# Order of the prefix in a four-layer graph network: edge fetch, row statistics, normalization and the first table products

## The chip, the cores and the metric

The kernel runs on one core of one Trainium2 chip, in one launch. The metric is device microseconds for the whole kernel. Engines are called as the profile calls them: PE (TensorE, matrix products; PEld is its weight load), DVE (VectorE), ACT (ScalarE), POOL (GpSimd) and SP (SyncE, which here only issues DMAs). ACT and POOL issue DMAs too.

## The reference, cut to what matters

A network of four layers works on x (1250 nodes, 512 features, float32) and 21250 edges sorted by target. Each layer adds three sublayers to x: one on the graph, one mixing all nodes, one of experts. The change touches only the start of layer 0, where the graph sublayer and the mixing sublayer read the same normalized x:

```
xn  = (x - mean) / sqrt(var + 1e-5)                    # per row
# graph (GATv2), k = 0, 1, 2; edges with loops, loop attribute = mean of incoming attributes
xl, xr = xn @ Wl[k] + bl[k], xn @ Wr[k] + br[k]        # two tables
m      = leaky_relu(xl[src] + xr[dst] + ef)            # per edge
alpha  = segment_softmax(m @ att[k], dst)
xn     = relu(layernorm(segment_sum(alpha * xl[src], dst) + b_out[k] + xn))
# mixing (linear attention) of the first xn
q, k, v = phi(xn Wq), phi(xn Wk), xn Wv                # phi = elu + 1, 8 heads
out     = (q (k^T v)) / (q . sum(k)) @ W_out + b_out
```

## The kernel before

Rows are kept in ten tiles of 128 (`NT` = 10, the last with 98 rows). x stays in the on-chip memory as `self.x`, `[128, 10, 512]`. A matrix product of one tile with a 512 x 512 weight is four matmuls in the text, each of which the profile shows as two, so eight per product.

**Two arms and a branch.** `count_edges` fetches the edge targets (`dsti`, and shifted by one `nexti`), and counts on DVE how many lie at or above each of 13 block borders (L273) and whether they are sorted (L275). A matmul with ones (L278) adds the counts over partitions into `ps`; L280 copies them to `tot`; L281 to L293 turn them into `flag`, which every engine loads. If it is zero the fast arm runs (`run(True)`), and that is what these inputs do; the other arm is in the program too. Nothing inside an arm can be issued ahead of the branch. `load_x` is called before `count_edges`, so SP issues x's two DMAs (L1571, L1573) ahead of those of the targets (L260, L262).

**The fast arm's first part** is `gat_first`, the function that the change edits most:

- `gat_vectors` and `gat_weights` issue DMAs for att, the weights `wl` and `wr`, and small vectors; L1120 to L1132 are POOL, ACT and SP work on `we` and `br`.
- `prepare_edges` (L314 to L453) assigns edges to 48 groups of 512 in `place_edges`, most of it small DVE instructions; one indirect DMA from POOL's queue (L431) fetches `raw`, the records of all edges; `take_edges` then fills `fields` with some twelve DVE instructions on 48 x 512. `turn_fields` transposes `fields` on PE (L523) into `rec`.
- `ready(t)` computes a tile's row statistics: L205, L206, L207 on DVE, a square root on ACT (L208). `norm_tile` (L221, L222) writes `xn`; L1537 stores it to `xtab` by ACT's DMA queue; `transpose_tile` (L160) writes `xnT`, evacuated by ACT (L134) and DVE (L136) in turn.
- `linear_attention_steps` is a generator. Its first `next` loads `wk`, `wv` and the vector `bo` and makes the K product of tile 0 (L171); later steps are the other K products, sums over nodes (L776), and the Q products, two yields each.
- `gat_tables` gives eight functions per tile, four for the product with `wl` and four with `wr` (L1161); after the fourth of each the result is evacuated (L1169 to L1179) and stored by SP. The local generator `steps` yields after each product: 20 table products, then the rest of the attention.
- `onehot_steps` makes, for each of 47 groups, a one-hot matrix from `rec` on DVE (L550), four transposes (L557) and four small products (L568) on PE, and stores. The loop around it takes one step of `steps` for each group. `clear` (L1721, L1723, L1725) zeroes buffers in memory.
- `mean_edges` (L597 to L633) forms means of the edge attributes, which need all 47 groups.

When all of this is over, other on-chip buffers are opened and `gatv2_fast` begins with indirect DMAs on POOL (L231) that gather table rows per edge.

**What sets the order.** The text is not the order of issue. Every instruction gets a rank from its place in the text; a planner with its own model of costs then writes one queue for each engine, taking at each moment the instruction of best rank that its model says can start. On the chip each engine works through its queue in order and waits where a dependence isn't met yet. So moving lines changes ranks, and the queues follow as far as the planner's model lets them.

Of the kernel before, what the change touches and what calls it, by code (L numbers as in the profile page):

```python
# [25 lines left out]
NT = 10  # L26
# [31 lines left out]
class Net:  # L58
# [193 lines left out]
    def count_edges(self):  # L252


        nc, c = self.nc, self.const
        self.given = c.tile([128, NB], F32, name="given")
        self.before = c.tile([128, NB], F32, name="before")
        with self.tc.tile_pool(name="prep0", bufs=1, side="right") as t1:
            dsti = t1.tile([128, ED], I32, name="dsti")
            nc.sync.dma_start(dsti, self.I["dst1"])  # L260
            nexti = t1.tile([128, ED], I32, name="nexti")
            nc.sync.dma_start(nexti, self.I["dst1n"])  # L262
            dst = t1.tile([128, ED], F32, name="dst")
            nc.vector.tensor_copy(dst, dsti)
            nxt = t1.tile([128, ED], F32, name="nxt")
            nc.vector.tensor_copy(nxt, nexti)
            one = t1.tile([128, ED], F32, name="one")
            nc.vector.memset(one, 1.0)

            cnt = t1.tile([128, NB + 2], F32, name="cnt")  # L270
            junk = t1.tile([128, ED], F32, name="junk")
            for b in range(NB + 1):
                nc.vector.scalar_tensor_tensor(junk, dst, float(b * BN), one, op0=ALU.is_ge,  # L273
                                               op1=ALU.mult, accum_out=cnt[:, b:b + 1])
            nc.vector.scalar_tensor_tensor(junk, dst, 0.0, nxt, op0=ALU.max, op1=ALU.is_gt,  # L275
                                           accum_out=cnt[:, NB + 1:])
            ps = self.tp([128, NB + 2])
            nc.tensor.matmul(ps, lhsT=self.ones, rhs=cnt, start=True, stop=True)  # L278
            tot = t1.tile([128, NB + 2], F32, name="tot")
            nc.vector.tensor_copy(tot, ps)  # L280
            nc.vector.tensor_tensor(self.given, tot[:, :NB], tot[:, 1:NB + 1],  # L281
                                    op=ALU.subtract)

            room = t1.tile([128, NB], F32, name="room")
            nc.vector.memset(room, float(4 * 128 * GE - BN))
            nc.vector.memset(room[:, NB - 1:], float(3 * 128 * GE - (N - (NB - 1) * BN)))
            over = t1.tile([128, NB + 1], F32, name="over")
            nc.vector.tensor_tensor(over[:, :NB], self.given, room, op=ALU.is_gt)
            nc.vector.tensor_copy(over[:, NB:], tot[:, NB + 1:])
            odd = t1.tile([128, 1], F32, name="odd")  # L290
            nc.vector.tensor_reduce(odd, over, AX.X, ALU.add)
            flag = t1.tile([1, 1], I32, name="flag")
            nc.vector.tensor_copy(flag, odd[0:1])  # L293
            nc.vector.tensor_scalar(self.before, tot[:, :NB], tot[:, 0:1], -1.0,
                                    op0=ALU.subtract, op1=ALU.mult)
            return nc.values_load(flag[0:1, 0:1], min_val=0, max_val=128 * ED + NB)
# [1224 lines left out]
    def gat_first(self, pv, xtab):  # L1521
        nc, I = self.nc, self.I
        L = self.gat_vectors(0, pv)
        with self.tc.tile_pool(name="l0", bufs=1) as p, \
                self.tc.tile_pool(name="l0tab", bufs=2) as pt:
            xn = p.tile([128, NT, D], F32, name="xn")
            xnT = p.tile([128, 4, NP], F32, name="xnT")
            with self.tc.tile_pool(name="edge", bufs=1, side="right") as pe, \
                    self.weights(), self.psum(4, 3, 1):
                self.edge_pool = pe  # L1530
                self.gat_weights(L, pt)
                self.prepare_edges()
                for t in range(NT):
                    self.ready(t)
                for t in range(NT):
                    self.norm_tile(t, xn[:, t, :])
                    nc.scalar.dma_start(xtab[t * 128:(t + 1) * 128, :], xn[:, t, :])  # L1537
                    self.transpose_tile(xnT[:, :, t * 128:(t + 1) * 128], xn[:, t, :])
                self.turn_fields(range(6))
                nc.vector.tensor_copy(self.srcI, self.rec[:, :, 0])  # L1540

                attention = self.linear_attention_steps(
                    xn, xnT, I["L0_mix_W_qkv"], I["L0_mix_W_out"], I["L0_mix_b_out"], 1.0,
                    lambda o, d: nc.vector.tensor_scalar(o, d, 1e-6, None, op0=ALU.add))
                next(attention)

                def steps():
                    for t in range(NT):
                        for i, f in enumerate(self.gat_tables(
                                L, pt, t, lambda c: xnT[:, c, t * 128:(t + 1) * 128])):  # L1550
                            f()
                            if i % 4 == 3:
                                yield
                    yield from attention

                steps = steps()
                for i, _ in enumerate(self.onehot_steps()):
                    next(steps, None)
                    if i == 20:
                        self.clear(pt)  # L1560
                self.mean_edges()
                for _ in steps:
                    pass
        with self.psum(4, 2, 2):
            self.gatv2_fast(L, xtab)

    def load_x(self, src):
        nc = self.nc
        nc.vector.memset(self.x[:, NT - 1, :], 0.0)
        main = (NT - 1) * 128  # L1570
        nc.sync.dma_start(self.x[:, :NT - 1, :],  # L1571
                          src[:main, :].rearrange("(t p) d -> p t d", p=128))
        nc.sync.dma_start(self.x[:LAST, NT - 1, :], src[main:, :])  # L1573

    def layer0_ffn(self):
# [1548 lines left out]
```

## Time and profile before

| | us |
|---|---|
| median of 3 runs (lowest to highest) | 4618.6 (4614.17 to 4620.98) |
| the profiled execution | 4626.03 |
| its span | 4624.2 |
| PE busy | 3950.4 (85%) |
| DVE busy | 2760.3 (60%) |
| ACT busy | 1506.7 (33%) |
| POOL busy | 1361.1 (29%) |

The span is the time from the first to the last recorded instruction. Busy shares are means over many stages with different limits; the part in question is the first 312 us, up to the first gather, and the sections below read it by stretches and by the timeline. In the profile's lines a name such as `xn` stands for all tiles of that name, and a line number can be that of a helper (L160, L171, L205) which many callers share. `x<-xn` at L1537 is the store to `xtab`. A matmul's end is modelled, so a busy PE is not PE at its peak.

### The profile page before, as it was taken

To read this page: it belongs to the slowest core of one execution; us is meant where nothing else is said; L and a number is where in the kernel's file an instruction comes from. 1 tells how busy PE (TensorE), PEld (TensorE's weight loads), DVE (VectorE), ACT (ScalarE), POOL (GpSimd) and SP (SyncE) were. 2 spreads that over 40 slices of the span, in tenths; PEclk is the share of its full clock that TensorE was granted. 3 is DMA by queue.
4 is the path that set the end of the run, shared out by engine and by line. 5 is a ranking of instruction groups with operands and counts; after the bars stand their busy time and mean duration, and the time that the engine had idled before them with its cause. 6 is when DMAs were issued, how large, how long until landed. Compare 5 with 4: busy or idle time off the path is not lost.

```text
span 4624.2 us, 49180 instructions
## 1 busy us (share of the span) xinstructions
PE 3950.4 (85%) x15439; PEld 2438.3 (53%) x15454; DVE 2760.3 (60%) x6534; ACT 1506.7 (33%) x2738; POOL 1361.1 (29%) x1198
## 2 busy tenths in 40 slices
PE   6978997899878876799899999997969975898796
PEld 3435553455444443444788877564536553454574
DVE  5358884888488966533796767314693135587301
ACT  2213332343233355111374346222221022455121
POOL 2026663566356501101100000103253003676101
PEclk9998998899989977899999999998989997998798
DMA  6446664566456612411521110382011285565695
GB/s 221 149 124 193 183 190 140 165 185 190 128 168 180 172 63 77 139 33 35 161 65 41 56 34 28 138 318 95 12 54 62 73 271 164 156 202 175 234 339 191
DMA packets 282999, 647.56 MB, mean 140 GB/s; under 512 B 61673, under 2 KB 108905, under 8 KB 267322
## 3 DMA queue, kind: packets, MB, share of 16 engines
q1 hardware_dynamic: 169290, 357.13, 23.7%
q0 software_dynamic: 73088, 234.75, 18.0%
q10 hardware_dynamic: 40352, 52.44, 3.4%
q8 instruction: 126, 2.06, 0.2%
q14 instruction: 143, 1.17, 0.1%
HBM read 528.87 MB, written 120.65 MB: 140 GB/s over the span
## 4 chain that ended last, share of the span: by engine, by line
PE 32%; DVE 9%; DMA 5%; issue 3%; ACT 2%; POOL 1%; SPq 0%; another core or an unknown queue 0%; ACTq 0%; POOLq 0%; DVEq 0%
PE more L2051 5%; PE mm L2601 4%; PE mm L1914 3%; PE mm L179 3%; PE mm L171 3%; PE mm L3039 2%; DMA xe<-routed_in 2%; PE mm L776 2%; PE mm L2295 2%; PE mm L2013 1%; PE more L2877 1%; PE mm L2290 1%; DVE junk L1942 1%; DVE e L1976 1%; PE mm L2405 1%
## 5 line engine op out<-in xcount | busy, mean ns | idle before, releaser
L231 POOL DMA_INDIRECT xl<-xl,srcI x564 | 610.8, 1083 | 404.1 <-PE more L1325 167.6
L1325 PE MATMUL more<-xl,wT 128*128 128x512 f32 x1128 | 584.9, 611 | 5.5 <-ACT wT L1315 5.5
L1256 PE MATMUL mm<-hl,oh 121*128 121x512 f32 x564 | 399.1, 708 | 103.6 <-DVE s L1269 66.7
L1269 DVE TENSOR_TENSOR s<-xl,mm 128x512 f32<-128x512 f32 x540 | 364.0, 680 | 170.2 <-PE mm L1257 80.8
L1272 DVE SCALAR_TENSOR_TENSOR junk<-s,att 128x512 f32<-128x512 f32 x540 | 405.0, 750 | 5.5
L2051 PE MATMUL more<-hh,e 128*128 128x259 f32 x1600 | 384.2, 386 | 11.7 <-ACT o L1994 9.4
L2051 PEld LDWEIGHTS more<-hh,e 128*128 128x128 f32 x1600 | 295.0, 191 | 76.3 <-issue 16.0
L171 PE MATMUL mm<-w,xnT 128*128 128x512 f32 x640 | 307.0, 619 | 13.8 <-DVE xnT L136 5.3
L231 POOL DMA_INDIRECT g<-routed_out,getI x60 | 66.5, 1109 | 681.5 <-DMA routed_out<-o 494.7
L1325 PEld LDWEIGHTS more<-xl,wT 128*128 128x128 f32 x1128 | 207.0, 196 | 92.2 <-issue 44.2
L1257 PE MATMUL mm<-hl,oh 121*128 121x512 f32 x564 | 242.5, 430 | 0.0
L231 POOL DMA_INDIRECT hs<-gcn_h,srcI x188 | 213.5, 1136 | 95.6 <-issue 35.5
L1256 PEld LDWEIGHTS mm<-hl,oh 121*128 121x128 f32 x564 | 112.6, 200 | 226.9 <-issue 115.2
L1243 ACT ACTIVATE oh<-nb 112x512 fp32r<-112x512 bf16 x141 | 88.6, 629 | 356.1 <-DMA nb<-nbt 241.9
L171 PEld LDWEIGHTS mm<-w,xnT 128*128 128x128 f32 x640 | 123.4, 198 | 141.9 <-issue 125.2
L1971 ACT ACTIVATE e<-r,hh 128x512 f32<-128x512 f32 (+1 forms) x240 | 154.1, 646 | 131.8 <-PE more L2051 120.9
L2601 PE MATMUL mm<-form,cw 128*128 128x312 f32 (+1 forms) x640 | 175.5, 436 | 21.8 <-POOL cw L2578 18.2
L2877 PE MATMUL more<-hl,oh 128*128 128x512 f32 x376 | 162.0, 532 | 35.0 <-DVE hl L2838 9.8
L1974 ACT ACTIVATE e<-r,a 128x512 f32<-128x512 f32 (+1 forms) x240 | 152.3, 646 | 70.6 <-DVE e L1976 58.5
L1976 DVE TENSOR_TENSOR e<-e,e 128x512 f32<-128x512 f32 (+1 forms) x240 | 141.6, 596 | 50.9 <-ACT e L1971 44.6
L1315 ACT COPY wT<-tp 128x512 f32<-128x512 f32 x141 | 82.3, 584 | 267.4 <-PE tp L1312 212.8
L160 PE MATMUL tp<-ident,xn 128*128 128x128 f32 x280 | 51.4, 331 | 135.2 <-issue 56.2
(618 smaller groups left out, 7894.0 us busy)
## 6 DMA issues: line engine op xcount, KB each, us to landing
w<-L_ffn_Wp SPq DMA_DIRECT2D x64, 1024.0 KB
w<-L_ffn_table SPq DMA_DIRECT2D x56, 1025.0 KB
neg<-ntab SPq DMA_DIRECT2D x80, 320.0 KB
nb<-nbt SPq DMA_DIRECT2D x141, 128.0 KB
hl<-xr SPq DMA_DIRECT2D x36, 448.0 KB
xr<-tro SPq DMA_DIRECT2D x30, 512.0 KB
xe<-routed_in SPq DMA_DIRECT2D x56, 256.0 KB
routed_out<-o ACTq DMA_DIRECT2D x56, 256.0 KB
```

What stands on the lines that cost most here:

```text
L171: self.nc.tensor.matmul(p, lhsT=xT[:, c, t * 128:(t + 1) * 128], rhs=w[:, c, n0:n0 + n], start=c == 0, stop=c == k - 1)
L231: self.nc.gpsimd.indirect_dma_start(out=out, out_offset=None, in_=table, in_offset=bass.IndirectOffsetOnAxis(ap=idx, axis=0), bounds_check ...
L1256: nc.tensor.matmul(m, lhsT=s, rhs=hl[:K, 0, :], start=True, stop=False)
L1257: nc.tensor.matmul(m, lhsT=s, rhs=hl[:K, 1, :], start=False, stop=not on_pe(i))
L1269: nc.vector.tensor_tensor(o, d["xl"][:, j, :D], s, op=ALU.add)
L1272: nc.vector.scalar_tensor_tensor(junk, s, 0.0, L["att"], op0=ALU.max, op1=ALU.mult, accum_out=d["lg"][:, j:j + 1])
L1325: nc.tensor.matmul(B[b]["y"], lhsT=d["wT"][:, j, :], rhs=d["xl"][:, j, :D], start=k == 0 and j == 0, stop=last and j == GE - 1)
L1971: nc.scalar.activation(e1[:, :n], R[q, k, 0][:, :n], AF.Exp, bias=HH[q][:, s, 256:257])
L1976: nc.vector.tensor_tensor(e1[:, :n], e1[:, :n], e2[:, :n], op=ALU.max)
L2051: nc.tensor.matmul(ys[j], lhsT=e[:, j * 128:(j + 1) * 128], rhs=HH[q][:, s, :], start=s == 0, stop=s == NT - 1)
L2601: nc.tensor.matmul(m, lhsT=g[:, which, c, :], rhs=forms[form][:, c, q % 2, q // 2:q // 2 + n], start=j + c == 0, stop=j + 1 == len(gs) and ...
L2877: nc.tensor.matmul(y, lhsT=oh, rhs=hl[:, i], start=i + j == 0 and not (self.fast and k), stop=last and i + j == GE)
```

## The change

- `load_x` is called inside `count_edges`, after the two DMAs of the targets, and fetches x in three pieces of three tiles and one of the last tile, in place of one piece of nine tiles and one of the last.
- `ready(t)` for all ten tiles stands in `count_edges`, after the matmul that adds the counts and ahead of the copy of its result, in place of its old place in `gat_first` after `prepare_edges`.
- In `gat_first` the ten tiles are normalized, stored and transposed first. Two steps of `steps` follow (`wl` and `wr` of tile 0), the first step of the attention, two more steps (tile 1), and then `prepare_edges`, one more step, `turn_fields` and the copy to `srcI`. Before, `prepare_edges` stood ahead of the statistics, and `turn_fields` and `srcI` ahead of the attention's first step and of all of `steps`.

No arithmetic is added or removed.

```diff
@@ count_edges
             nexti = t1.tile([128, ED], I32, name="nexti")
             nc.sync.dma_start(nexti, self.I["dst1n"])
+            self.load_x(self.I["x"])
             dst = t1.tile([128, ED], F32, name="dst")
...
             nc.tensor.matmul(ps, lhsT=self.ones, rhs=cnt, start=True, stop=True)
+            for t in range(NT):
+                self.ready(t)
             tot = t1.tile([128, NB + 2], F32, name="tot")
@@ gat_first
                 self.gat_weights(L, pt)
-                self.prepare_edges()
-                for t in range(NT):
-                    self.ready(t)
                 for t in range(NT):
                     self.norm_tile(t, xn[:, t, :])
                     nc.scalar.dma_start(xtab[t * 128:(t + 1) * 128, :], xn[:, t, :])
                     self.transpose_tile(xnT[:, :, t * 128:(t + 1) * 128], xn[:, t, :])
-                self.turn_fields(range(6))
-                nc.vector.tensor_copy(self.srcI, self.rec[:, :, 0])
-
                 attention = self.linear_attention_steps(
...
-                next(attention)
 
                 def steps():
...
                 steps = steps()
+                for _ in range(2):
+                    next(steps)
+                next(attention)
+                for _ in range(2):
+                    next(steps)
+                self.prepare_edges()
+                next(steps)
+                self.turn_fields(range(6))
+                nc.vector.tensor_copy(self.srcI, self.rec[:, :, 0])
                 for i, _ in enumerate(self.onehot_steps()):
@@ load_x
-        nc.sync.dma_start(self.x[:, :NT - 1, :],
-                          src[:main, :].rearrange("(t p) d -> p t d", p=128))
+        for t in range(0, NT - 1, 3):
+            nc.sync.dma_start(self.x[:, t:t + 3, :], src[t * 128:(t + 3) * 128, :]
+                              .rearrange("(t p) d -> p t d", p=128))
@@ kernel
-        net.load_x(I["x"])
         with net.psum():
             odd = net.count_edges()
```

## The prediction

> **What bounds the kernel now.** I read the page first, then the busy time in stretches, the timeline of the first 320 us by engine, and the table of waits there. The chain of waits reaches back only to 2215 us, so for the prefix (everything ahead of the first gather of the graph layers) the stretches have to say what sets its end. The stretches (length, busy time per engine with instruction counts, granted clock, DMA share, GB/s):
>
> ```profile
> 0.00:10.00 10.00, 0.00 (x0) 0.00 (x0) 1.88 (x13) 0.00 (x0) 0.51 (x6) 1.00 0.76 260
> 10.00:20.00 10.00, 0.61 (x2) 0.50 (x2) 6.73 (x41) 0.00 (x0) 0.75 (x2) 1.00 0.06 13
> 20.00:30.00 10.00, 0.00 (x0) 0.00 (x0) 7.84 (x46) 2.30 (x6) 3.98 (x5) 1.00 0.93 303
> 30.00:40.00 10.00, 4.36 (x8) 2.23 (x9) 6.99 (x18) 1.09 (x4) 1.18 (x2) 1.00 0.97 257
> 40.00:50.00 10.00, 3.55 (x9) 1.44 (x7) 10.00 (x17) 0.41 (x2) 6.65 (x3) 0.88 0.37 137
> 50.00:60.00 10.00, 8.68 (x35) 5.71 (x36) 9.45 (x18) 2.60 (x5) 8.77 (x7) 0.78 0.50 186
> 60.00:70.00 10.00, 9.38 (x51) 4.95 (x50) 7.08 (x13) 6.32 (x11) 4.75 (x4) 1.00 0.41 145
> 70.00:80.00 10.00, 8.93 (x50) 4.38 (x49) 5.04 (x11) 2.85 (x5) 2.29 (x2) 1.00 0.67 242
> 80.00:250.00 170.00, 170.00 (x718) 83.51 (x717) 62.87 (x119) 48.91 (x89) 0.00 (x0) 1.00 0.49 167
> 250.00:312.00 62.00, 57.24 (x162) 27.07 (x160) 33.16 (x68) 11.22 (x20) 0.96 (x1) 0.94 0.22 57
> ```
>
> The first busy column is TensorE. From 80 to 250 us it is busy 170.00 of 170 us at clock 1.00, while VectorE is busy 62.87: there the prefix is bound by matmuls that follow each other without a gap. Before 80 us TensorE is mostly empty and VectorE is nearly full. So the prefix ends earlier by as much TensorE time as the change fills ahead of 80 us. The timeline gives the marks (start, duration, instruction, the idle time before it and who ended it):
>
> ```profile
> 11.25 0.25 DVE L264 CAST dst<-dsti 128x168 f32<-128x168 int32 x1 [8.31 <-DMA dsti<-dst]
> ...
> 18.38 0.14 DVE L293 CAST flag<-odd 1x1 int32<-1x1 f32 x1
> ...
> 26.31 1.39 POOL L431 DMA_INDIRECT raw<-etab,edgeI  x1 [6.01 <-DVE mr L365]
> ...
> 36.53 0.61 DVE L444 CAST fields<-raw 48x512 f32<-48x512 int32 x1 [3.01 <-DMA raw<-etab,edgeI]
> ...
> 36.73 5.71 PE L171 MATMUL mm<-w,xnT 128*128 128x512 f32 x8 [4.54 <-DMA w<-L_mix_W_qkv]
> ...
> 64.36 1.29 DVE L550 TENSOR_TENSOR ohb<-iota_free,rec 128x512 bf16<-128x512 f32 x2
> ```
> ```profile
> 275.14 1.24 PE L523 MATMUL tp<-ident,fields 48*128 48x48 f32 x8 [4.71 <-DVE fields L621]
> ...
> 312.90 1.03 POOL L231 DMA_INDIRECT xl<-xl,srcI  x1 [42.43 <-DVE big L1191]
> ```
>
> The edge targets arrive at 11.25 behind x's 2.3 MB; the branch opens at 19.3 (POOL L351, DVE L314); wk lands at 36.7; the first one-hot starts at 64.36; the first gather waits for VectorE, which ends the prefix at 312. Everything later hangs on that gather, and I assume it moves with it.
>
> **TensorE time left empty before.** In the plateau a 512-column product (8 matmuls) takes 3.68, so one matmul 0.46. At that speed the work done by 80 us is: one K product 3.7; 40 transposes of xn at 8 in 1.06, 5.3; 24 transposes of fields at 12 in 0.94, 1.9; 38 table matmuls 17.5; five one-hot groups at 0.39 + 0.25, 3.2. Sum 31.6, so 48.4 of the 80 us are lost.
>
> **Fetch order and the branch.** The targets (168 KB) go ahead of x. I take them as landed at about 4 us: at 0.74 a first DMA issues, and the DMA engines carry nothing before about 1.5. The counting of 11.25 to 16.79 (5.5 us) then ends at 9.5 and its matmul (0.6) at 10.1. Ten row statistics at 0.68 + 0.16 + 0.13 = 0.97 cost 9.7 us on VectorE. They stand in the text ahead of the copy of the totals; if they stay ahead of it in VectorE's queue, as I assume where x has landed, the totals begin at 19.8, the flag follows 1.0 later (17.49 to 18.52 now), the branch 0.75 after that: 21.5 instead of 19.3, a loss of 2.2 for everything in the branch that isn't VectorE. Other end: the flag slips in ahead of them and the branch opens at 12. The ten square roots (0.20 each, one table load 1.28) lie beside VectorE's work on ScalarE and cost nothing; without that cover, at most 3.3. x in four DMAs instead of two adds two issues at 0.45 on an SP queue with nothing else to send. The tile of zeros in x costs VectorE 0.48 either way.
>
> [...]
>
> **Weights.** Now wk lands 17.2 us after SP's first issue at 19.54. In between go att (0.26 MB), wl, wr, wk (1.05 each), the raw edge records (0.59) and one 0.26 MB store of xn: 4.25 MB at the 280 GB/s of 20 to 40 us is 15.2. After the change up to ten such stores by ScalarE's queue fall into that time. Lower bound without raw: 17.2 - 2.1 = 15; upper with nine more stores: 17.2 + 2.36 MB / 280 GB/s = 25.6. From 21.8 wk lands between 37 and 47; I take 42, because normalizing tile by tile spreads the stores.
>
> [...]
>
> **Products ahead.** By 42 us TensorE has done the transposes (5.3), wl and wr of tile 0 (7.4): 12.7, so 29.3 is lost. Then K, wl and wr of tile 1 and wl of tile 2 follow: 4 x 3.68 = 14.7, to 57.
>
> **The edges, now later.** VectorE from 21.5: ten norms at 0.12 + 0.55 = 6.7, five evacuations 3.4, att 0.4, to 32. Placing 4.3, raw 10.2 (26.31 to 36.53 now, with the evacuations of the moved products, six at 0.7, inside that wait), the field arithmetic 11.4 (36.53 to 47.9 now), transposes and copies 2.6: the first one-hot at 60.5 instead of 64.4. Cheapest, without POOL beside it (0.67 instead of 1.46 for each L452): 57. Dearest, all of it at the doubled rates: 71. Between 57 and 60.5 TensorE has wr of tile 2 to do; I count half as lost, 1.8, and 1.5 for the start of the one-hots as now (8.93 of 10). Lost in all: 29.3 + 1.8 + 1.5 = 32.6.
>
> **Sum.** 48.4 - 32.6 = 15.8 us. The profiled execution took 4626.0 (span 4624.2), so 4610.2 on it; the median of three, 4618.6, becomes 4602.8. At 170 of 170 busy nothing between gives this back. The last one-hot (252.4 now) moves towards the end by some three products (five table products ahead instead of the 1.75 that TensorE had done by then), 11 us; the chain of means behind it ends at 275 with TensorE stalled 4.7, and 36 us of work follow: covered. What isn't moved by the text stays at nothing: no instruction is added, two DMAs are.
>
> **Rivals.**
> (a) The flag goes ahead of the statistics. For: POOL's memset L1721 (19.75) precedes L431 (26.31) though it is later in the text, so the queues are not in text order. Weights start 9 us earlier, VectorE stays as late as before: some 9 us more than the sum, 4594.
> (b) The one-hots set the end, not the matmuls. For: VectorE's one-hots wait 41.2 us on L568. Then only 64.4 - 60.5 = 3.9 is won: 4615. Against: 170 of 170 busy. A planner that had already filled the queues whatever the text says ends here too.
> (c) Slower: raw's gather is stuck on POOL. In-order behind L1125 (waits for br; 8.82 now) and the ten additions of b to x (L805, 14.0 us) that become ready once the norms are done, but need the bias vector, which lands after wv, 46 to 51 us. If they are queued ahead of L431, it starts at 60 to 65, not 36, or up to 6 later with L1125 (4.0) and L1128 (1.5) there too, and the one-hots at 84 to 95. Products beyond the moved ones cover some 5 of the 24 to 34 more; TensorE loses 19 to 29: 4622 to 4632, middle 4627, likelier above it, since L1125 already waits now. If the planner finds three further products (11 us) ahead of the fields' transposes, which TensorE takes in order, it is 4611 to 4616. It decides when the first one-hot is later than 76 (60.5 + 15.8). Against: raw stands earlier in the text than those additions, and now one addition comes only at 43.44.
>
> **Chances.** Forecast 0.50 (4594 to 4609); (a) 0.15; (b) 0.17; (c) 0.18, mostly its dear end. 0.2% is 9.2 us, about what a measurement of this kernel can tell from no change. All of the forecast and (a) lie below 4609.4: faster 0.65. (b) and the mild end of (c): same 0.22. The rest of (c), above 4627.8: slower 0.13. Range 4590 to 4628: below it only (a) with wk at its earliest, above it the dear end of (c).
>
> **What would show it.** First dst at 4 us, not 11; wl's first product before 35 us; 85% or more of TensorE busy from 42 us on; the first one-hot at 57 to 64; the first gather near 297. A first gather at 312 or later, L431 after 50 us, or a TensorE wait of over 5 us on fields would prove it wrong.

## The result, and the profile after

The changed kernel takes 4621.6 us (median of 19 runs, 4599.4 to 4647.3) against 4623.4 us of the kernel before in the same session (19 runs): ratio 0.9993 (estimated from all runs, so not the quotient of the two medians), 95% interval 0.9978 to 1.0007. In a second session it was 0.9984 (0.9970 to 0.9999). So it is faster by 0.22% at most by the first interval, by 0.30% at most by the second, where 0.34% was forecast; the two ratios stand for gains of 3 and 7 us, not 15.8. The profiled execution of the changed kernel took 4647.3 us (span 4645.5), the longest of its 19 runs; its prefix can be read, its end can't be held against that of before.

Line numbers behind the change have moved by 3 (L1161 is L1164, L431 is L434, L550 is L553, L805 is L808). First the stretches, with the columns as before (TensorE, its weight load, VectorE, ScalarE, POOL, granted clock, DMA share, GB/s):

```profile
20.00:30.00 10.00, 7.68 (x37) 5.23 (x36) 7.32 (x31) 1.80 (x4) 0.00 (x0) 0.83 1.01 364
30.00:40.00 10.00, 5.50 (x16) 2.27 (x13) 4.61 (x20) 1.17 (x2) 3.89 (x3) 0.91 1.03 282
40.00:50.00 10.00, 7.12 (x10) 3.09 (x11) 4.19 (x6) 1.69 (x3) 2.80 (x2) 0.57 0.55 180
50.00:60.00 10.00, 10.00 (x29) 4.40 (x28) 8.03 (x8) 3.39 (x5) 7.30 (x5) 1.00 0.15 37
60.00:70.00 10.00, 6.39 (x31) 3.63 (x30) 8.85 (x14) 2.50 (x5) 6.54 (x4) 0.78 0.43 160
70.00:80.00 10.00, 7.58 (x34) 3.34 (x33) 5.34 (x6) 1.85 (x4) 6.52 (x5) 0.88 0.44 160
80.00:250.00 170.00, 170.00 (x714) 83.69 (x714) 66.42 (x125) 48.76 (x89) 0.00 (x0) 1.00 0.48 168
```

Next to before, TensorE has filled 20 to 60 us (30.3 busy instead of 16.6), but in 60 to 80 us it is less busy than it was (14.0 instead of 18.3), and in 40 to 50 us its granted clock is 0.57. From 80 to 250 us it is full in both. The marks in the timeline:

```profile
2.69 0.25 DVE L265 CAST dst<-dsti 128x168 f32<-128x168 int32 x1 [0.34 <-DMA dsti<-dst]
...
16.40 0.14 DVE L296 CAST flag<-odd 1x1 int32<-1x1 f32 x1
...
42.88 6.49 PE L171 MATMUL mm<-w,xnT 128*128 128x512 f32 x8 [7.38 <-DMA w<-L_mix_W_qkv]
```
```profile
144.67 4.54 PE L779 MATMUL mm<-k,xn 128*128 128x512 f32 x10
```
```profile
283.63 1.23 PE L526 MATMUL tp<-ident,fields 48*128 48x48 f32 x8 [6.29 <-DVE fields L624]
```
```profile
308.22 1.04 POOL L231 DMA_INDIRECT xl<-xl,srcI  x1 [29.13 <-DVE big L1194]
```

The targets are there at 2.69 and the flag at 16.40, 2 us earlier than before. K's product (L171) waits 7.4 us for wk and then takes 6.49. The first sum of the attention over the nodes (L779, one fixed point of TensorE's plateau) comes at 144.67, before at 154.41: 9.7 us ahead. The line of before:

```profile
154.41 4.54 PE L776 MATMUL mm<-k,xn 128*128 128x512 f32 x10
```

At the first gather 4.7 are left (308.22 for 312.90), at the first mixing product of the graph layer (`more<-xl,wT`, L1328) 0.9 (371.78 for 372.64). Where the edges are late is seen on VectorE and POOL:

```profile
42.64 0.68 DVE L447 CAST fields<-raw 48x512 f32<-48x512 int32 x1 [5.44 <-DMA raw<-etab,edgeI]
...
51.97 0.69 DVE L751 SCALAR_TENSOR_TENSOR k<-mm,r 128x512 f32<-128x512 f32 x1 [5.13 <-ACT r L750]
...
53.18 1.75 DVE L453 TENSOR_TENSOR fields<-fields,e 48x512 f32<-48x512 f32 x1
54.86 3.99 DVE L455 TENSOR_TENSOR fields<-raw,m 48x512 f32<-48x512 f32 x2
...
59.38 3.36 DVE L455 TENSOR_TENSOR fields<-raw,m 48x512 f32<-48x512 f32 x2
62.78 1.60 DVE L456 TENSOR_TENSOR fields<-fields,loops 48x512 f32<-48x512 f32 x1
...
66.22 0.68 DVE L553 TENSOR_TENSOR ohb<-iota_free,rec 128x512 bf16<-128x512 f32 x1
```
```profile
32.10 1.40 POOL L434 DMA_INDIRECT raw<-etab,edgeI  x1 [12.77 <-DVE mr L367]
...
52.70 12.80 POOL L808 TENSOR_TENSOR x<-x,b 128x512 f32<-128x512 f32 x7 [7.59 <-DMA b<-L_mix_b_out]
68.97 1.81 POOL L545 TENSOR_TENSOR rest<-rec,parts 128x768 f32<-128x768 f32 x1 [3.46 <-DVE parts L544]
70.73 2.81 POOL L808 TENSOR_TENSOR x<-x,b 128x512 f32<-128x512 f32 x2
73.50 1.80 POOL L547 TENSOR_TENSOR rest<-rest,parts 128x768 f32<-128x768 f32 x1
```

The field arithmetic (L447 to L456) takes 21.7 us, 42.64 to 64.38; before it took 11.4. Between its operations stands K's phi (L751), which waits 5.1 us; and from 52.7 on POOL adds the mixing bias to x (L808) beside it. L453 and L456 take 1.75 and 1.60 instead of 0.65 to 0.67, and POOL's additions 1.83 each (12.80 / 7) instead of 1.26 for one that ran alone. Two lines of before:

```profile
47.27 0.65 DVE L453 TENSOR_TENSOR fields<-fields,loops 48x512 f32<-48x512 f32 x1
```
```profile
48.51 1.26 POOL L805 TENSOR_TENSOR x<-x,b 128x512 f32<-128x512 f32 x1 [3.13 <-DVE rsx L221]
```

In the changed kernel POOL then does two more additions between its two subtractions that split the fields (L545, L547), for which the one-hots' products wait. And wk is late because SP's queue stands still (waits: engine and line, what it waited for, total, times, longest; then the issue of wk, before and in the changed kernel):

```profile
SPq L1125 <- DMA w<-L_gnn_Wr: 4.8, 1, 4.8
SPq L1121 <- DMA w<-L_gnn_Wl: 4.1, 1, 4.1
SPq L1120 <- DMA att<-L_gnn_att: 2.7, 1, 2.7
```
```profile
21.82 0.39 SPq L141 DMA_DIRECT2D w<-L_mix_W_qkv  x1
```
```profile
32.70 0.40 SPq L141 DMA_DIRECT2D w<-L_mix_W_qkv  x1
```

The three waits are those of fetches and stores of 2 to 32 KB, put in SP's queue ahead of wk; each waits until an earlier large fetch has landed. In the trace of this run the DMAs of SP and ScalarE up to 55 us share eight completion semaphores (a semaphore is the counter that tells of a landing): the fetch of `we` waits for and takes over that of att, the fetch of `bl` that of wl, the store of `br` that of wr. The ten stores of xn by ScalarE use up the others. So wk was issued at 32.7, not at 21.8 as before.

### The profile page after: what moved, and what is told of

Its sections match the earlier page's. It is cut to its first block, busy times and chain, and to the rows that moved or that the text cites. A ratio compares the mean times of both kernels' runs of the same rounds, so it can differ in the third digit from the quotient of the medians.

```text
span 4645.5 us, 49184 instructions
## 1 busy us (share of the span) xinstructions
PE 3969.4 (85%) x15439; PEld 2455.6 (53%) x15454; DVE 2766.2 (60%) x6534; ACT 1508.3 (32%) x2738; POOL 1364.4 (29%) x1198
## 4 chain that ended last, share of the span: by engine, by line
PE 39%; DVE 9%; DMA 6%; issue 3%; ACT 2%; POOL 1%; SPq 1%; another core or an unknown queue 0%; ACTq 0%; POOLq 0%; DVEq 0%
PE mm L171 5%; PE mm L179 5%; PE more L2057 5%; PE mm L2607 4%; PE mm L1920 3%; PE mm L3045 2%; DMA xe<-routed_in 2%; PE mm L779 2%; PE mm L2301 2%; PE more L2883 1%; PE mm L2296 1%; PE mm L2019 1%; PE tp L160 1%; DVE junk L1948 1%; DVE e L1982 1%
## 5 line engine op out<-in xcount | busy, mean ns | idle before, releaser
L1328 PE MATMUL more<-xl,wT 128*128 128x512 f32 x1128 | 578.0, 605 | 3.7 <-ACT wT L1318 3.7
L2057 PEld LDWEIGHTS more<-hh,e 128*128 128x128 f32 x1600 | 293.7, 190 | 77.0 <-issue 15.8
L171 PE MATMUL mm<-w,xnT 128*128 128x512 f32 x640 | 307.1, 619 | 16.6 <-DMA w<-L_mix_W_qkv 7.4
L1328 PEld LDWEIGHTS more<-xl,wT 128*128 128x128 f32 x1128 | 205.5, 194 | 87.4 <-issue 41.6
L171 PEld LDWEIGHTS mm<-w,xnT 128*128 128x128 f32 x640 | 123.2, 198 | 144.2 <-issue 119.9
L2883 PE MATMUL more<-hl,oh 128*128 128x512 f32 x376 | 165.8, 545 | 32.6 <-issue 13.5
L1980 ACT ACTIVATE e<-r,a 128x512 f32<-128x512 f32 (+1 forms) x240 | 152.2, 646 | 71.9 <-DVE e L1982 59.7
L1286 PE MATMUL tp<-ident,lg 128*128 128x128 f32 x564 | 95.0, 292 | 86.1 <-DVE lg L1282 58.0
```

Of the source, the lines that this page charges most:

```text
L171: self.nc.tensor.matmul(p, lhsT=xT[:, c, t * 128:(t + 1) * 128], rhs=w[:, c, n0:n0 + n], start=c == 0, stop=c == k - 1)
L1328: nc.tensor.matmul(B[b]["y"], lhsT=d["wT"][:, j, :], rhs=d["xl"][:, j, :D], start=k == 0 and j == 0, stop=last and j == GE - 1)
L2057: nc.tensor.matmul(ys[j], lhsT=e[:, j * 128:(j + 1) * 128], rhs=HH[q][:, s, :], start=s == 0, stop=s == NT - 1)
L2883: nc.tensor.matmul(y, lhsT=oh, rhs=hl[:, i], start=i + j == 0 and not (self.fast and k), stop=last and i + j == GE)
```

## The experiments

Theory: POOL's additions, now beside the edges' chain, and wk's late issue leave TensorE waiting or at a low clock (0.57 from 40 to 50 us); the chain of means takes some of the lead back; what is left is too small for the time to show. Rivals: full DMA engines hold wk back; the shift doesn't reach the end. A mark at the first gather repeats to 1 to 6 us, a time ratio to about 0.0015 (7 us). All marks in us, one profile each; "table matmuls" are those of L1164 (its number differs by a few lines from kernel to kernel) done by 80 us; each ratio is to the kernel before, run beside it.

| kernel | first one-hot | table matmuls | first sum | first gather | first mixing product | ratio to before, 95% |
|---|---|---|---|---|---|---|
| before | 64.4 | 38 | 154.4 | 312.9 | 372.6 | 1 |
| before, again | 64.8 | 37 | 154.8 | 314.1 | 372.4 | |
| changed | 66.2 | 58 | 144.7 | 308.2 | 371.8 | 0.9993 (0.9978 to 1.0007) |
| changed, again | 61.3 | 60 | 143.9 | 306.3 | 369.5 | 0.9984 (0.9970 to 0.9999) |
| before, branch part only | 54.8 | 41 | 152.5 | 312.1 | 370.7 | 0.9985 (0.9970 to 1.0001) |
| changed, weights first | 65.9 | 65 | 141.8 | 304.7 | 362.3 | 0.9980 (0.9963 to 0.9996) |
| changed, means late | 57.4 | 65 | 141.3 | 300.6 | 367.5 | 0.9992 (0.9977 to 1.0007) |
| changed, additions late | 57.5 | 83 | 132.8 | 295.1 | 352.9 | 0.9972 (0.9962 to 0.9982) |
| the same, again | 61.2 | 75 | 136.6 | 300.7 | 359.1 | 0.9957 (0.9940 to 0.9973) |
| weights first, additions late | 55.4 | 87 | 130.8 | 293.8 | 351.7 | 0.9959 (0.9943 to 0.9975) |
| additions late, means late | 61.0 | 75 | 136.4 | 296.4 | 366.7 | 0.9965 (0.9949 to 0.9981) |
| all three | 56.0 | 86 | 131.3 | 291.3 | 358.0 | 0.9967 (0.9951 to 0.9982) |
| before, additions late | 59.0 | 49 | 149.0 | 308.3 | 369.8 | 0.9975 (0.9958 to 0.9992) |
| changed, delayed | 63.2 | 61 | 143.2 | 330.6 | 376.6 | 1.0021 (1.0001 to 1.0042) |

### Both kernels once more

No edit. 

> The changed kernel once more, so that marks of one profile can be told from accidents of one execution. Theory (T): the marks of the prefix are set by the order of the queues and repeat to within 0.5 us: wk's product at 42.9, first one-hot 66.2, first sum of the attention 144.7, first gather 308.2. The lead of 4.7 us over the kernel before at the first gather is real, and what the profiled execution lost after 2300 us (it ended 20 us late) is not repeated. Rival (accident): the profiled execution was slow throughout and this one has its first gather at 297 to 303. Time: 0.999 to 1.001 of the kernel before under T, 0.996 under the rival.

> The kernel before once more, the same question from the other side: first one-hot 64.4, first gather 312.9, first mixing product of the graph layer at 372.6, last gather of the third graph pass at 1602, each within 0.5 us up to the first gather. If the marks behind 372 us scatter by more than 3 us between executions of one kernel, a lead of 3 us there can't be followed by single profiles.

The lead at the first gather repeats: 306.3 and 308.2 against 312.9 and 314.1. But the marks from 40 to 66 us don't repeat to 0.5 us: K's product began at 39.3 here, 42.9 there, as wk landed earlier or later, and the first one-hot followed (61.3 and 66.2). Nor does the first gather, to better than 2 us. The time, 0.9984, lies between what theory and rival gave.

### The branch part alone

```diff
 (before)
+            self.load_x(self.I["x"])      # in count_edges, behind the targets; x in pieces
...
+            for t in range(NT):           # in count_edges, ahead of the totals
+                self.ready(t)
...
                 self.prepare_edges()      # gat_first: order unchanged
-                for t in range(NT):
-                    self.ready(t)
```

> The kernel before with the first half of the change alone: targets fetched first, x in pieces, row statistics ahead of the branch; normalization, products and edges stay in the old order. Theory (T): the branch opens 2 us earlier (17.3, not 19.25) and VectorE has 5 to 8 us less to do between the branch and the edges, so the edges come earlier than in either kernel: raw issued at 24, first one-hot at 60 to 62, first gather 309 to 311; all of that half's gain is kept, and the second half (products ahead) adds 2 to 3 us at the first gather. Rival (the second half is the loss): first gather at 306 or earlier, ahead of the full change, so that moving the products cost time. Time: 0.999 to 1.000.

The first one-hot came at 54.8, 10 us earlier than before, and the first gather at 312.1, 1 to 2 us earlier: both theories were off, and early one-hots by themselves are worth little: TensorE had only three more table matmuls done by 80 us (41 for 38). By the time (0.9985) this half can't be told from the whole change in the same session (0.9984). Two lines each of VectorE and POOL, then the cast to srcI in the kernel before:

```profile
47.50 7.35 DVE L1541 CAST srcI<-rec 128x192 int32<-128x192 f32 x1
54.77 1.75 DVE L553 TENSOR_TENSOR ohb<-iota_free,rec 128x512 bf16<-128x512 f32 x1
```
```profile
47.29 1.27 POOL L1131 TENSOR_TENSOR wehl<-we,wehl 3x512 fp32r<-3x512 f32 x1
48.52 7.45 POOL L808 TENSOR_TENSOR x<-x,b 128x512 f32<-128x512 f32 x6
```
```profile
64.11 0.30 DVE L1540 CAST srcI<-rec 128x192 int32<-128x192 f32 x1
```

The cast to srcI, 0.30 us before, takes 7.35 here: it ends when POOL's row of seven operations ends (55.97), but for one us. POOL's stayed at 1.24 each. TensorE waits 7.5 us for the copy of `rec` that VectorE has behind this cast, and its first transposes of one-hots start at 57.1.

### The weights first

```diff
 (changed; gat_weights)
         L["wr"] = self.weight(I["L0_gnn_Wr"][k], 4, D)
+        if early is not None:          # the parts of W_qkv for wk and wv
+            L["kv"] = [self.weight(w, 4, D) for w in early]
         v = p.tile([128, D], F32, tag="v", name="we")
...
 (linear_attention_steps)
-            wk = self.weight(w_qkv[:, D:2 * D], 4, D)
-            wv = self.weight(w_qkv[:, 2 * D:3 * D], 4, D)
+            wk, wv = kv or [self.weight(w_qkv[:, i * D:(i + 1) * D], 4, D) for i in (1, 2)]
```

> The changed kernel with wk and wv put straight behind wl and wr in SP's queue, ahead of the small fetches we, bl and br that wait there for earlier DMAs. The same bytes flow, the xn stores included. Theory (T, the queue held wk back): wk is issued at 22 to 25 us instead of 32.7, its product starts at 35 to 38 instead of 42.9, its phi on VectorE is done before the raw records land (42.6), so the 5.1 us that VectorE waited there are gone: first one-hot at 60 to 62 instead of 66.2, first sum of the attention at 138 to 141 instead of 144.7, first gather 302 to 305. Rival (the DMA engines are full: share 1.01): wk lands at 41 to 44 wherever it stands in the queue, and all marks stay as in the changed kernel within 1 us; then wl or wr land later instead. Time: 0.997 to 0.999 under T, 0.999 to 1.001 under the rival.

The queue was the cause, not full engines: with the same bytes wk was issued at 21.7 and its product took 3.70 after a wait of 0.56, where the changed kernel has 6.49 after 7.38, while the products of wl began when they did there (26.3 and 26.2). The kernel with the weights first and the additions late, whose K product began at 36.13, has a DMA share of 1.02 from 20 to 40 us, the changed one 1.01 and 1.03. But the one-hots came no earlier. The K product on TensorE, POOL's additions and what follows them, ScalarE's copy of wehl, and TensorE's wait:

```profile
35.91 3.70 PE L171 MATMUL mm<-w,xnT 128*128 128x512 f32 x8 [0.56 <-DMA w<-L_mix_W_qkv]
...
44.53 16.42 POOL L807 TENSOR_TENSOR x<-x,b 128x512 f32<-128x512 f32 x10 [8.21 <-DMA b<-L_mix_b_out]
60.92 1.25 POOL L1129 TENSOR_TENSOR we<-we,br 3x512 f32<-3x512 f32 x1
```
```profile
62.20 0.62 ACT L1131 CAST wehl<-we 3x512 fp32r<-3x512 f32 x1 [18.53 <-POOL we L1129]
...
64.34 0.66 PE L526 MATMUL tp<-ident,fields 48*128 48x48 f32 x4 [10.84 <-ACT rec L134]
```

All ten additions now stand ahead of the sum that wehl needs (L1129): ScalarE waits 18.5 us for it, with the evacuation of a field transpose queued behind, and TensorE is empty for 10.8 us. The second wait took the place of the first. The first gather (304.7) and the time are as the theory had them, the first sum (141.8) is just past it.

### The additions late

```diff
 (changed; linear_attention_steps, ahead of the loop over the tiles)
             Q, QT = {}, {}
+            if added is None:
+                nc.vector.scalar_tensor_tensor(bo, ks, 0.0, bo, op0=ALU.mult, op1=ALU.add)
```

> The changed kernel with the ten additions of the bias vector to x on POOL made to wait until the attention's column sums ks are there: one VectorE operation (0.7 us) writes b + 0*ks in place of b. Nothing else moves in POOL's queue. Theory (T: POOL's additions beside VectorE's field arithmetic doubled it, L455 at 2.0 and 1.7 each, L453 and L456 at 1.6 to 1.75): L455 takes 1.0 each, L456 0.7, the casts L546 and L548 0.55 instead of 1.6, and POOL's subtractions L545 and L547 come without the additions between them; first one-hot 3 to 6 us earlier than in the changed kernel (56 to 61), TensorE busy 31 of the 40 us up to 80 becomes 34 or more, first sum of the attention at 140 to 142 instead of 144, first gather 303 to 305. Rival (VectorE's durations have another cause, such as the transfers): L455 stays at 1.7 to 2.0 and no mark moves. Second rival: the additions only move the trouble to 220 to 280 us, where POOL's gather of the means (L617) stands behind them: TensorE's stall at 283 grows over 7 us. Time: 0.997 to 0.999.

In this kernel the ten additions of L808 move behind POOL's subtractions, and the order on SP, ScalarE and TensorE stays the same up to the graph layer. VectorE, then POOL:

```profile
48.99 0.68 DVE L453 TENSOR_TENSOR fields<-fields,e 48x512 f32<-48x512 f32 x1
49.59 2.04 DVE L455 TENSOR_TENSOR fields<-raw,m 48x512 f32<-48x512 f32 x2
...
52.15 2.05 DVE L455 TENSOR_TENSOR fields<-raw,m 48x512 f32<-48x512 f32 x2
54.24 0.68 DVE L456 TENSOR_TENSOR fields<-fields,loops 48x512 f32<-48x512 f32 x1
...
57.46 0.68 DVE L553 TENSOR_TENSOR ohb<-iota_free,rec 128x512 bf16<-128x512 f32 x1
...
62.05 0.56 DVE L546 CAST parts<-rest 128x768 bf16<-128x768 f32 x1 [1.93 <-POOL rest L545]
...
64.53 0.56 DVE L548 CAST parts<-rest 128x768 bf16<-128x768 f32 x1 [1.32 <-POOL rest L547]
```
```profile
60.20 1.81 POOL L545 TENSOR_TENSOR rest<-rec,parts 128x768 f32<-128x768 f32 x1 [14.97 <-DVE parts L544]
62.69 1.80 POOL L547 TENSOR_TENSOR rest<-rest,parts 128x768 f32<-128x768 f32 x1 [0.67 <-DMA l0moe_in<-zero]
...
201.22 13.65 POOL L810 TENSOR_TENSOR x<-x,b 128x512 f32<-128x512 f32 x10 [136.72 <-DVE b L806]
```

L453 and L456 are back at 0.68, the casts L546 and L548 at 0.56, and POOL's subtractions follow each other 2.5 us apart, not 4.5. L455 stays at 1.02, so that part of its length isn't POOL's. The additions cost nothing at 201 us, and TensorE's stall in the tail is 6.26 us, not more. The table products by 80 us, changed kernel and this one (matmuls, busy time, mean ns of one):

```profile
L1164 PE MATMUL mm<-w,xnT 128*128 128x512 f32 x58 | 30.7, 669 | 0.0
```
```profile
L1166 PE MATMUL mm<-w,xnT 128*128 128x512 f32 x83 | 38.7, 603 | 0.0
```

25 matmuls more, at 0.47 us each by busy time (38.7 / 83) instead of 0.53 (30.7 / 58); the means of the view are longer because matmuls overlap (83 of 0.603 are 50.0 us, in 38.7 busy). First sum and first gather:

```profile
132.81 4.54 PE L779 MATMUL mm<-k,xn 128*128 128x512 f32 x10
```
```profile
295.12 1.03 POOL L231 DMA_INDIRECT xl<-xl,srcI  x1 [27.84 <-DVE x L185]
```

That is more than the theory said (140 to 142 and 303 to 305): it named the splitting, but its 3 to 6 us were for the first one-hot, ahead of it. The first gather is 17.8 us ahead of before, and the time 0.9972. The repetition:

> The changed kernel with the additions late once more, for a narrower interval beside the other three on one chip: first gather at 294 to 297, first mixing product at 351 to 358, time 0.9965 to 0.998. If the first gather is back at 304 or later, the first run's marks were an accident of one execution, and POOL's additions aren't the cause.

With wk late in this execution (TensorE waited 7.1 us for it, 3.6 in the first), the marks are 4 to 6 us later, past the expected ranges. From the first sum on they are still 5 us or more ahead of the changed kernel; the first one-hot is not (61.2 for 61.3 to 66.2). The time is 0.9957, below the expected range. Against the changed kernel's two ratios the two of this kernel are lower by 0.0012 to 0.0036, 6 to 17 us, with intervals that touch.

### Weights first and additions late

The diffs are those of the two sections above, together.

> Both edits together: wk and wv fetched straight behind wl and wr, and POOL's ten additions made to wait for ks. With the weights first alone, TensorE was busy 25 to 52 us, and then empty for 13 us (52 to 65): the right table's evacuation waited on ScalarE for wehl, which waited on POOL behind all ten additions (16.4 us, 44.5 to 61), and the one-hots were no earlier (65.9). Theory (T: each of the two alone leaves the other's wait standing): first one-hot at 53 to 57, TensorE empty for under 5 us between 25 and 80 us, first sum of the attention at 133 to 137 (144 in the changed kernel, 141.8 with weights first), first gather 296 to 300; that is the gain that the prediction put on the change (15.8 us at the first gather, of 312.9), with the stall of the means still in it. Rival (they overlap: the one-hots or the raw records set the pace): first sum at 139 or later, first gather 301 or later. Time: 0.9955 to 0.9975 under T.

All marks are as expected or earlier. TensorE is empty for 3.5 us between 25 and 80 us. Against the additions late alone the first sum gains 2 to 6 us, the time nothing that can be told (0.9959).

### The means late

```diff
 (changed; mean_edges)
-            self.turn_fields((2, 3))
+            if not self.fast:
+                self.turn_fields((2, 3))
...
 (gat_first)
                 for _ in steps:
                     pass
+                self.turn_fields((2, 3))
```

> The changed kernel with the transposes of the two mean fields (L526, which waited 6.3 us on VectorE's L624 with TensorE idle behind them) moved behind the last attention product. Theory (T: nearer the end the chain of means is no longer covered): the stall of 6.3 us at 283 us and the low clock after it (0.53 in 280 to 290) are gone; first gather at 299 to 302 instead of 306.3 to 308.2, of which the first gather keeps all. Rival (something else holds the end: the means' own gather and VectorE's fields are needed by the first gather or by what follows at once): first gather stays at 305 to 308, or moves and the first mixing product of the graph layer stays at 369 to 372. Time: 0.9965 to 0.9985 under T, as the changed kernel (0.9984) under the rival.

The transposes wait no longer, and the first gather is at 300.6:

```profile
299.64 0.69 PE L526 MATMUL tp<-ident,fields 48*128 48x48 f32 x8
```

Part of that is an early first sum (141.3). The fair measure is the stretch from first sum to first gather: 158.5 and 159.3 before, 163.6 and 162.4 changed, 159.3 here. So the means' stall took back 3 to 5 us, net of a wait of 3.9 us for q (L160 at 285.62) that stands in its place. But the first mixing product is at 367.5, 67 us after the gather (58.2 to 59.7 before, 63.2 and 63.6 changed), and the time is 0.9992: the part of the theory that all of it is kept fell.

> The changed kernel with the additions late and the transposes of the two mean fields behind the last attention product. With the additions late alone TensorE still waited 6.3 us on the means' fields (at 272 us) and the stretch from the first sum of the attention to the first gather was 162.3 us, as in the changed kernel (162.4 to 163.5; before 158.5 to 159.3; with the means late 159.3). Theory (T: the means' stall is worth 3 to 4 us of this stretch): first sum at 132 to 134, first gather 290 to 293, stretch 158 to 160. Rival (something else of the attention's end sets it, such as the copies of q): stretch 162 or more. Time: 0.9955 to 0.9975.

The stretch is 160.0, as expected; the first sum was late (136.4, wk again landed late), and again the first mixing product came late, 70 us after the gather.

> All three edits on the changed kernel: wk and wv straight behind wl and wr, additions late, transposes of the mean fields last. Theory: they add up, as each takes away a wait of its own: first sum of the attention at 130 to 132, first gather 288 to 291, first mixing product of the graph layer at 345 to 350 (before 372.5). Rival (the first mixing product is held by transfers that don't move): 352 or later. Time: 0.995 to 0.997.

First gather 291.3, the earliest of all, but the first mixing product 67 us later, at 358.0: past the rival's 352. (That transfers hold it, the rival's reason, isn't shown.) In all three kernels with this edit that stretch is 67 to 70 us; in the four other profiles with the weights first or the additions late on the changed kernel it is 57.6 to 58.4. What the edit wins at the gather is lost on the way to that mark. Which wait does it, I haven't isolated.

### The same edit on the kernel before

The diff is that of the additions late, applied to the kernel before.

> The kernel before with the same single edit as in the changed kernel: POOL's ten additions of the bias vector to x wait until the attention's ks is there. It asks whether the 11 to 13 us that the edit brought in the changed kernel belong to the edit alone or to the edit and the change together. Theory (T: the change laid the edges' chain, VectorE's field arithmetic and the splitting of the fields, beside those additions; before, most of them fell beside the normalization, 48 to 63 us, and ended before POOL's subtractions L542 at 68.7): the field arithmetic loses some 2 us (L452 1.0 each, not 1.6) and the normalizations their doubled rows (1.3 to 0.53, some 4 us), so first one-hot at 58 to 61 instead of 64.4 and first gather 307 to 310 instead of 312.9 to 314.1; time 3 to 6 us less (0.9985 to 0.9995). So of the changed kernel's 12 to 13 us at the first gather, 7 or more are the change's own, that the additions had hidden. Rival (the edit is a gain of its own): first gather at 302 or earlier, 0.9975 or less, and the change is worth little with or without it.

The marks are where the theory put them: first one-hot 59.0, first gather 308.3. The time, 0.9975, lies at the rival's bound, with the theory's 0.9985 inside its interval. By the marks, then, the additions cost 5 to 6 us at the first gather in the kernel before and 6 to 13 in the changed one, and with them out of the way the change brings the first gather from 308.3 to 295.1 and 300.7, 8 to 13 us. By the time, 0.9957 and 0.9972 against 0.9975, that rest is not settled: the intervals overlap.

### A delay

```diff
 (changed; gat_first, behind the attention)
+                last = self.x[:, NT - 1, :]
+                for _ in range(40):
+                    nc.vector.tensor_scalar(last, last, 1.0, None, op0=ALU.mult)
+                zero = pv.tile([128, 1], F32, name="zero")
+                nc.vector.tensor_scalar(zero, last[:, 0:1], 0.0, None, op0=ALU.mult)
+                nc.vector.tensor_scalar(self.srcI, self.rec[:, :, 0], zero, None, op0=ALU.add)
```

> The changed kernel with 40 operations of VectorE in a row (x's last tile times 1.0, 0.55 us each, 22 us in all) between the last addition of the attention and the sources' copy that the first gather reads. It asks what a us at the first gather is worth at the end. Theory (T: all behind hangs on that gather): first gather at 328 to 332, first mixing product at 391 to 395, time 22 us over the changed kernel: ratio to the kernel before 1.002 to 1.005. Second theory (the start of the graph layer swallows some 4 us, as the lead of 4.7 us had become 0.8 to 2 us at the first mixing product): 17 to 18 us, 1.001 to 1.004, not to be told from the first by the time but by the mark at the first mixing product (386 to 389). Rival (a shift of the prefix doesn't reach the end): 0.998 to 0.9995.

```profile
330.56 1.02 POOL L231 DMA_INDIRECT xl<-xl,srcI  x1 [4.60 <-DVE srcI L1574]
```

The first gather is 22 to 24 us later than in the changed kernel, and the ratio 0.0032 above the mean of its two (0.99885), 15 us; the interval of the delayed one alone is some 9.5 us to either side, and that of the changed kernel adds to it. So a shift at the first gather does reach the end; whether all of it does, or two thirds, or less, the noise hides. The first mixing product moved by only 5 to 7 us, to 376.6, where the theories had 386 or later: that single mark isn't a price for the end either.

## Why the prediction was wrong, step by step

- **Fetch order and branch.** Targets 4 forecast, 2.69 measured; branch 21.5 forecast, 17.3 measured. The statistics were queued between the countings, not in a block ahead of the totals. Neither the forecast's order nor rival (a); worth 4 us on the good side. With x in pieces the DMAs moved 268 GB/s in the first 10 us instead of 260, and VectorE nowhere waits for x.
- **Weights.** wk at 42: K's product began at 42.9 and 39.3. The number held, its reason (bytes of the xn stores ahead of it) didn't: the weights first brought it to 35.9 with the same bytes. The DMA share is 1.01 and 1.03 from 20 to 40 us with K's product at 42.9, and 1.02 with it at 36.1 (weights first, additions late): what held wk was its place in SP's queue.
- **TensorE time left empty.** 32.6 forecast; 80 less 46.6 busy gives 33.4 (31.2 in the second profile). The sum fits partly by luck: up to K's product 27.4 are empty for 29.3 forecast, behind it 6.0 for 3.3 (82% busy from 42 us on, where 85% was the sign). And the work done by 80 us is not the forecast's 47.4. At the plateau's prices it is K 3.7, transposes 5.3 and 1.9, 58 table matmuls at 0.46, 26.7, three one-hot groups 1.9: 39.5, so 7.9 gained over before's 31.6, half of 15.8. **This is the step that failed**: "lost in all: 29.3 + 1.8 + 1.5 = 32.6" counts empty time alone and takes every busy us at full clock. Of 46.6 busy us, 7.1 did no work at these prices; 0.6 of them are the counting matmul (L279), the rest went into the low clock (busy time times the clock missing, summed over the stretches shown, is 7.2). In before's 48.4, 3.9 of that kind stood under "lost" (35.5 busy for 31.6 of work); the sum for after had no such term. With the additions late, 54.9 busy us did 52.9 of work (83 matmuls, six groups).
- **The edges, now later.** First one-hot 60.5 forecast, 66.2 and 61.3 measured. The field arithmetic was taken at before's 11.4; it took 21.7 and 16.3. The doubled rates were in the dear bound (71). The cheap bound's 0.67 for each L452 wasn't reached with the additions late either (1.02). What the step missed is that the move itself puts this arithmetic where the bias vector lands, 46 to 51 us by rival (c)'s own row. The splitting behind it (L545 to L548) had only the 1.5 us "as now"; with POOL's additions there, TensorE was busy 14.0 of the 20 us from 60 on, with them late 18.2.
- **"170 of 170 busy nothing gives this back".** True for the plateau. The 9.7 us at the first sum are, roughly, the 7.9 of work and five one-hot groups that now stand behind that sum (20 ahead of it instead of 25; 3.2 at the prediction's price).
- **"36 us of work follow: covered".** Wrong: the work that followed stood behind the means' transposes in TensorE's queue and didn't run in the stall (6.3 instead of 4.7 us), and the clock was 0.53 around it (280 to 290 us). 3 to 5 us were given back, as the means late show.
- **"Everything later moves with it".** The delay shows that a shift reaches the end, some 15 of 22 to 24 us with an uncertainty of more than 9. The stretch from the first gather to the first mixing product differs by up to 13 us between the kernels without the delay (57.6 to 70.3) and isn't explained here.
- **Rivals.** (b) is refuted by the branch part alone: one-hots 10 us earlier, first gather 1 to 2. That its gain of 3.9 us lies between the measured 3 and 7 is luck. (c) named the right instructions and the wrong queue: raw's gather was not behind the additions (L434 at 32.1), VectorE was beside them. Its time would have been 4622 to 4632; the forecast put 0.18 on it.

## What to carry to other kernels

When work is moved earlier, list what the other engines will be doing at its new place, above all small operations that were free to run whenever their input landed, and give them a dependency that sends them to a stretch where their engine is idle: one VectorE operation, put into the kernel before, did as much at the first gather (5 to 6 us) as the whole reordering (5 to 8). Count the work that an engine gets done, not its busy time: here K's product took 6.49 us after a wait of 7.38, and 3.70 after one of 0.56. And look for small DMAs that wait for the semaphore of an earlier large one: here three such waits (2.7, 4.1 and 4.8 us) held wk, behind them in SP's queue, by 11 us.

## What was not expected of the hardware

- Operations of VectorE and POOL took longer side by side, without a common datum: VectorE's 48x512 operations L453 and L456 1.75 and 1.60 us beside POOL's additions, 0.68 with the additions late; POOL's 128x512 additions 1.83 beside VectorE's field arithmetic, 1.26 for one alone. And a 128x192 cast, 0.30 us in the kernel before, took 7.35 in the branch part alone, beside a row of POOL operations that stayed at 1.24 to 1.27. By these times the cast looks held through some six operations in a row, not run at a shared rate; that is my estimate, and what holds it isn't shown.
- The eight matmuls of K's product took 5.2 to 6.7 us after waits of 3.0 to 7.5 us (ten profiles), and 3.70 after waits of 0.4 to 1.2 (three). The granted clock was 0.50 in 40 to 45 us of the changed kernel's second profile, behind a wait of 3.3, and 1.00 in 20 to 40 us with the weights first and the additions late, around a wait of 1.15. Whether the wait lowers the clock, and from what length on, no run isolates.
- One program's executions differ by 3.5 us in when wk lands (K's product at 42.88 and 39.34), and its time by up to 48 us (4599 to 4647), about ten times what the change is worth.
